# A softmax lookup convolution: three lookups of every slot between its logits and its numerators

## The chip, the cores and the metric

The kernel runs on one core of a Trainium2 chip. A core has five engines that run at the same time, each through its own list of instructions, and wait for one another through semaphores: TensorE (PE in the profile) multiplies matrices, VectorE (DVE), ScalarE (ACT) and GpSimd (POOL) work on elements, SyncE (SP) issues transfers. TensorE writes into PSUM, an accumulator memory of eight banks, from which VectorE or ScalarE must read the results before a bank can be written again.

The metric is the device time of one execution in microseconds (us), as the median of several.

## The reference, cut to what matters

The input has 16 images of 256 channels of 28 x 28 pixels. Each image is normalized by groups of 8 channels and goes through two "lookup convolutions". In such a convolution every channel has 16 centroids of 9 values. The 3 x 3 neighbourhood of a pixel in this channel is compared with the 16 centroids; a softmax over the negative squared distances gives 16 weights; the weighted mean of the centroids takes the place of the neighbourhood and is multiplied by the convolution's weights.

```python
def amm_conv3x3(x, centroids, w_sub):
    p = ...  # 9 neighbours of every pixel and channel: [B, N, C, 9]
    d = sum(p * p) - 2 * einsum('bncs,cks->bnck', p, centroids) + sum(centroids ** 2)
    attn = softmax(-d, axis=-1)                         # over the 16 centroids
    lut = einsum('cks,cso->cko', centroids, w_sub)
    return einsum('bnck,cko->bno', attn, lut)

out = amm_conv3x3(group_norm(x), centroids1, wsub1)
out = relu(batch_norm1(out))
out = amm_conv3x3(out, centroids2, wsub2)
out = batch_norm2(out)
out = squeeze_and_excite(out)
return x + relu(out + group_norm(x))
```

The kernel doesn't build `lut`. It computes the 16 exponentials of a channel, from them nine numerators (exponentials times centroids) and their sum, divides, and multiplies the nine quotients by `w_sub`. All is in fp32.

## The kernel before

The 256 channels are split into eight tiles of 32 channels (index m), and the 784 pixels into two parts of 384 and 400. One tile and one part are the work of one *slot*: there are 16 images x 2 convolutions x 2 parts x 8 tiles = 512 slots. In a slot TensorE makes three kinds of product:

- logits: 16 small products of 32 x 32 tiles, from patches `pt` and codes `wd` into two pairs of PSUM banks
- numerators: 16 small products, from the exponentials `e` and `cw` into two further pairs
- lookups: products of full width, from `q` (the quotients) and `ws` into the accumulators `acc0` and `acc1`; 36 for eight slots, so four or five a slot

Each product is two matmul records in the profile. PSUM's eight banks are two accumulators and a ring of three pairs:

```python
ring = [p_ring.tile([P, 2, 512], F32, name=f"pair{i}") for i in range(3)]
turn = [0]

def pair():
    turn[0] += 1
    return ring[turn[0] % 3]

def logits(u, rows):
    l, n = u["l"], u["px"][1]
    ps = [pair(), pair()]
    for t in range(4):
        for i in range(4):
            c = 32 * ctile(i, t)
            nc.tensor.matmul(                                       # L563
                ps[t // 2][c : c + 32, t % 2, :n],
                lhsT=wd[l][32 * i : 32 * i + rows, 4 * u["m"] + t, :],
                rhs=u["pt"][32 * i : 32 * i + rows, t, :n],
                start=True, stop=True,
            )
    return ps
```

What follows the logits of a slot, in the order of the data: two exponentials on ScalarE, one a pair; the numerators; two transposes and a reciprocal on VectorE; the division on GpSimd, for k and for the ninth row `tail`; a transpose back on VectorE; and, three slots later, the lookups.

```python
def b_exp(u):
    ...
    for ps in u.pop("lg"):
        e = epool.tile([P, 2, 400], F32, tag="e", name="e")
        nc.scalar.activation(e[:, :, :n], ps[:, :, :n], AF.Exp, scale=2.0)      # L621
        u["e"].append(e)

def b_num(u):
    ...
    u["nm"] = [pair(), pair()]
    for t in range(4):
        for i in range(4):
            c = 32 * ctile(i, t)
            nc.tensor.matmul(                                       # L631
                u["nm"][t // 2][32 * i : 32 * i + 32, t % 2, :n],
                lhsT=cw[l][c : c + 32, 4 * u["m"] + t, :],
                rhs=es[t // 2][c : c + 32, t % 2, :n],
                start=True, stop=True,
            )

def b_turn(u):
    ...
    for v, ps in enumerate(u.pop("nm")):
        nc.vector.transpose(nt[...], ps[...])                       # L643
    nc.vector.reciprocal(rc[:, : 8 * nb], u["nt"][:, :, SUM])       # L649
    ...

def c_scale(u):   # GpSimd: k = nt * rc (L659), tail (L665), extremes of sums (L671)
def c_turn(u):    # VectorE: q = transpose of k (L677), every fourth slot qt of tail (L684)
def c_look(u, o, h):
    ...
    nc.tensor.matmul(                                               # L695
        accs[key][:, :n], lhsT=ws[l][...], rhs=u["q"][h][:, :n], start=first, stop=last,
    )
    if last:
        evacuate(u, o, accs.pop(key))    # ScalarE: L707, L717
```

A plan puts every job into a slot and, in the slot, at a position; jobs are then issued in this order:

```python
LC = 3
LOOKS = [(m, o, h) for m in range(NQ) for o in range(2) for h in range(3 if m % 4 == 3 else 2)]
LOGITS, LOAD, MOVE, EXP, LOOK_A, NUM, TURN, SMALL, LOOK_B, MAX, LOOK_C, TURN_BACK, REST = range(13)
...
slots = [n0 + (LC + q) * self.step for q in range(NQ)]
more = [2 if (s, MAX) in self.jobs else 0 for s in slots]
k, room = 0, len(LOOKS) - sum(more)
for q, s in enumerate(slots):
    n = (q + 1) * room // NQ - q * room // NQ + more[q]
    for i, (m, o, h) in enumerate(LOOKS[k : k + n]):
        self.at(s, LOOK_A if i < n // 2 + n % 2 - more[q] // 2
                   else LOOK_B if i < n - more[q] else LOOK_C, c_look, of[m], o, h)
    k += n
```

So TensorE's order in a slot is logits, lookups A, numerators, small products (of the statistics and the gate), lookups B. In the second convolution the tiles 0 and 4 need the maximum of their logits ahead of time. For them logits are made six slots earlier at position MAX, and VectorE transposes them (z) and takes the maximum; such a slot gets two lookups more, at C, behind those early logits.

The number of lookups of a slot and how they lie before the change, over the whole run:

| lookups of the slot | A + B + C before | slots |
|---|---|---|
| 4 | 2 + 2 | 350 |
| 5 | 3 + 2 | 98 |
| 6 (early logits) | 2 + 2 + 2 | 34 |
| 7 (early logits) | 3 + 2 + 2 | 30 |

Of the kernel before, what the change touches and what calls it, by code (L numbers as in the profile page):

```python
# [69 lines left out]
def kernel(  # L70
# [655 lines left out]
    LOGITS, LOAD, MOVE, EXP, LOOK_A, NUM, TURN, SMALL, LOOK_B, MAX, LOOK_C, TURN_BACK, REST = range(13)  # L726

    class Plan:
# [13 lines left out]
        def emit(self):  # L742

            free = [-99] * len(pts)
            for slot, last, u in sorted(self.loads, key=lambda v: v[:2]):
                tile = free.index(min(free))
                assert free[tile] <= slot
                free[tile] = last
                self.at(slot, LOAD, patches, u, tile)
            for n0, of in self.tiles:  # L750
# [4 lines that stand above are left out]
                for q, s in enumerate(slots):  # L755
                    n = (q + 1) * room // NQ - q * room // NQ + more[q]
                    for i, (m, o, h) in enumerate(LOOKS[k : k + n]):
                        self.at(s, LOOK_A if i < n // 2 + n % 2 - more[q] // 2 else LOOK_B if i < n - more[q] else LOOK_C, c_look, of[m], o, h)
                    k += n
            for key in sorted(self.jobs):  # L760
                for f, a in self.jobs[key]:
                    f(*a)
# [234 lines left out]
```

## Time and profile before

| | before |
|---|---|
| median time of 3 runs | 2973.09 us (2972.99 to 2977.15) |
| span of the profiled run | 2969.2 us |
| mean granted TensorE clock | 0.989 |
| TensorE busy (matmul records) | 2871.6 us, 97% |
| VectorE busy | 2252.7 us, 76% |
| GpSimd busy | 1768.5 us, 60% |
| ScalarE busy | 1092.7 us, 37% |

A line of the groups gives the source line, the engine, the operation, what is written from what, the shapes, the number of instructions, then the busy time in us and the mean of one in ns, and last the engine's idle time ahead of them and what ended most of it. A line of the timeline gives the start in us, the time from the first start to the last end, the engine, the line and the operation, and how many instructions in a row it stands for; a wait ahead of it stands in brackets with what ended it. In the view of waits a line names who waited, for whom, the total in us, the times and the longest. Matmul records overlap, as TensorE is pipelined, and a record that stands inside a block of others is counted as busy time of the block.

### The profile page before, as it was taken

What the parts mean: (1) busy time and instruction counts of PE and PEld (TensorE: products, weight loads), DVE (VectorE), ACT (ScalarE), POOL (GpSimd) and SP (SyncE); (2) the same over time, 40 slices, a digit from 0 to 9 for tenths busy, and PEclk for the clock granted to TensorE, in tenths of its full rate; (3) what the DMA queues carried; (4) which work ended last, traced back from release to release, by engine and by line L of the source; (5) the groups of instructions that cost most, each with busy time, mean ns of one, the idle gap of its engine ahead of it and who ended that gap; (6) DMA issues with size and microseconds to landing.
All of it is one profiled execution on the core that took longest, in us unless ns stands there. A gap on an engine that the chain in (4) does not pass through costs nothing.

```text
span 2969.2 us, 94838 instructions
## 1 busy us (share of the span) xinstructions
PE 2871.6 (97%) x39834; PEld 1145.4 (39%) x39834; DVE 2252.7 (76%) x2760; ACT 1092.7 (37%) x1605; POOL 1768.5 (60%) x2583
## 2 busy tenths in 40 slices
PE   4999999999999999999999999999999999999995
PEld 2433333333333333333333333333333333334332
DVE  3476777787877878787787877878788787878884
ACT  1332343433434343343433434343343434333332
POOL 3474575666656566665656656566665656656553
PEclk8999999999999999999999999999999999999998
DMA  6877777767767676776767667676776767674641
GB/s 185 227 174 170 203 219 195 212 154 213 186 169 197 151 208 174 197 185 154 211 156 207 180 180 188 154 214 156 214 185 163 200 155 206 177 189 106 163 114 56
DMA packets 296773, 530.30 MB, mean 179 GB/s; under 512 B 94240, under 2 KB 251664, under 8 KB 296336
## 3 DMA queue, kind: packets, MB, share of 16 engines
q0 software_dynamic: 51648, 269.78, 34.9%
q1 hardware_dynamic: 242512, 251.70, 32.7%
q8 instruction: 316, 5.18, 0.7%
q10 hardware_dynamic: 2176, 2.65, 0.3%
q14 instruction: 121, 0.99, 0.1%
HBM read 269.96 MB, written 254.05 MB: 176 GB/s over the span
## 4 chain that ended last, share of the span: by engine, by line
PE 79%; DMA 7%; DVE 6%; POOL 4%; issue 2%; ACT 2%; SPq 0%; ACTq 0%; DVEq 0%; POOLq 0%
PE acc L695 47%; PE pair L631 16%; PE pair L563 14%; DMA xt<-in_x 4%; DVE nt L643 2%; POOL k L659 2%; DVE rc L649 1%; DVE gn_st L417 1%; POOL total L671 1%; DMA pt<-pat 1%; ACT e L621 1%; DMA ws<-dws 1%; PE pair L309 0%; PE pair L324 0%; DVE q L677 0%
## 5 line engine op out<-in xcount | busy, mean ns | idle before, releaser
L695 PE MATMUL acc<-q,ws 128*128 128x384 f32 (+1 forms) x4096 | 1641.0, 519 | 9.7 <-ACT y L717 9.7
L659 POOL TENSOR_TENSOR k<-nt,rc 128x832 f32<-128x832 f32 (+1 forms) x512 | 802.3, 1567 | 1132.9 <-DVE rc L649 1120.5
L643 DVE STREAM_TRANSPOSE nt<-pair 128x832 f32<-128x832 f32 (+1 forms) x1024 | 976.3, 992 | 603.5 <-PE pair L631 506.4
L621 ACT ACTIVATE e<-pair 128x800 f32<-128x800 f32 (+1 forms) x1024 | 787.8, 821 | 1358.8 <-PE pair L563 1357.3
L695 PEld LDWEIGHTS acc<-q,ws 128*128 128x128 f32 x4096 | 696.9, 189 | 907.7 <-issue 577.2
L631 PE MATMUL pair<-e,cw 32*32 32x384 f32 (+1 forms) x16384 | 580.3, 502 | 11.9 <-ACT e L621 10.6
L563 PE MATMUL pair<-pt,wd 19*32 19x384 f32 (+2 forms) x18432 | 561.0, 500 | 5.9 <-DMA pt<-pat 3.3
L677 DVE STREAM_TRANSPOSE q<-k 128x832 f32<-128x832 f32 (+1 forms) x512 | 489.1, 955 | 0.8 <-POOL k L659 0.8
L649 DVE RECIPROCAL rc<-nt 128x104 f32<-128x104 f32 (+1 forms) x512 | 398.5, 778 | 17.6
L631 PEld LDWEIGHTS pair<-e,cw 32*32 32x32 f32 x16384 | 167.5, 103 | 349.2 <-ACT e L621 321.4
L563 PEld LDWEIGHTS pair<-pt,wd 19*32 19x32 f32 (+1 forms) x18432 | 138.4, 103 | 340.1 <-issue 265.5
L665 POOL TENSOR_TENSOR tail<-nt,rc 128x104 f32<-128x104 f32 (+1 forms) x512 | 242.4, 473 | 0.0
L695 PE MATMUL acc<-qt,ws 128*128 128x400 f32 (+1 forms) x512 | 218.6, 509 | 0.0
L671 POOL TENSOR_TENSOR total<-total,nt 128x96 f32<-128x96 f32 (+1 forms) x448 | 198.7, 443 | 0.0
L468 POOL DMA_DIRECT2D pat<-side x280 | 186.6, 667 | 1.1 <-DMA pat<-im 0.7
L671 POOL TENSOR_TENSOR total<-total,rc 128x96 f32<-128x96 f32 (+1 forms) x448 | 175.5, 392 | 0.0
L695 PEld LDWEIGHTS acc<-qt,ws 128*128 128x128 f32 x512 | 90.8, 189 | 100.1 <-issue 50.6
L587 DVE TENSOR_REDUCE mx<-z 128x48 f32<-128x768 f32 (+1 forms) x128 | 120.8, 943 | 0.0
L582 DVE STREAM_TRANSPOSE z<-pair 128x768 f32<-128x768 f32 (+1 forms) x128 | 119.2, 969 | 0.0
L468 POOL DMA_DIRECT2D pat<-im x140 | 94.0, 672 | 3.5 <-ACT im L447 3.5
L707 ACT ACTIVATE im<-acc,bnsh,bnsc 128x384 f32<-128x384 f32 (+1 forms) x64 | 43.4, 678 | 139.4 <-PE acc L695 133.4
L717 ACT ACTIVATE y<-acc,bnsh,bnsc 128x384 f32<-128x384 f32 (+1 forms) x64 | 43.4, 679 | 91.7 <-PE acc L695 76.8
(106 smaller groups left out, 753.5 us busy)
## 6 DMA issues: line engine op xcount, KB each, us to landing
pat<-side POOLq DMA_DIRECT2D x232, 588.0 KB, 6.1
pt<-pat SPq DMA_DIRECT2D x1024, 112.5 KB
pt<-pat SPq DMA_DIRECT2D x1024, 108.0 KB
pat<-im POOLq DMA_DIRECT2D x116, 588.0 KB, 5.3
xt<-in_x POOLq DMA_DIRECT2D x32, 784.0 KB, 8.8
out_dram<-y POOLq DMA_DIRECT2D x16, 784.0 KB, 4.0
pat<-side POOLq DMA_DIRECT2D x24, 300.0 KB, 6.1
pat<-side POOLq DMA_DIRECT2D x24, 288.0 KB, 6.0
```

Of the source, the lines that this page charges most:

```text
L468: nc.gpsimd.dma_start(view(pat, (ROWS * p0 + 9 * k + 3 * dx) * HW + px, [[ROWS * HW, m], [HW, 3], [1, n]]), bass.AP(v.tensor, v.offset, [l ...
L563: nc.tensor.matmul(ps[t // 2][c : c + 32, t % 2, :n], lhsT=wd[l][32 * i : 32 * i + rows, 4 * u["m"] + t, :], rhs=u["pt"][32 * i : 32 * i + ...
L587: nc.vector.tensor_reduce(u["mx"][:, 2 * v : 2 * v + 2].rearrange("p t (j b) -> p t b j", j=2)[:, :, :nb], u["z"].pop(0)[:, : 64 * nb].rea ...
L621: nc.scalar.activation(e[:, :, :n], ps[:, :, :n], AF.Exp, scale=2.0)
L631: nc.tensor.matmul(u["nm"][t // 2][32 * i : 32 * i + 32, t % 2, :n], lhsT=cw[l][c : c + 32, 4 * u["m"] + t, :], rhs=es[t // 2][c : c + 32, ...
L643: nc.vector.transpose(nt[:, :nb, 2 * v : 2 * v + 2].rearrange("p b t r -> p t b r"), ps[:, :, : 32 * nb].rearrange("p t (b r) -> p t b r", ...
L649: nc.vector.reciprocal(rc[:, : 8 * nb], u["nt"][:, :, SUM])
L659: nc.gpsimd.tensor_tensor(q[:, :nb].rearrange("p b (a s) -> p (b a) s", s=8), nt[:, :, :8], rc.unsqueeze(2).to_broadcast([P, 8 * nb, 8]), ...
L665: nc.gpsimd.tensor_tensor(tails[key][:, :nb, 8 * (m % 4) : 8 * (m % 4) + 8], nt[:, :, 8].rearrange("p (b a) -> p b a", a=8), rc.rearrange( ...
L671: nc.gpsimd.tensor_add(t[:, : 8 * nb], t[:, : 8 * nb], v)
L677: nc.vector.transpose(q[:, :, : 32 * nb].rearrange("p h (b r) -> p h b r", r=32), u.pop("k")[:, :nb].rearrange("p b (h r) -> p h b r", h=2),)
L695: nc.tensor.matmul(accs[key][:, :n], lhsT=ws[l][:, 2 * m + h if h < 2 else 2 * NQ + m // 4, o * P : (o + 1) * P], rhs=u["q"][h][:, :n], st ...
```

## The change

The change sets how many lookups lie between the logits and the numerators. Before, the lookups of a slot, without those behind early logits, were halved, and an odd one went ahead of the numerators. Now three always go ahead of the numerators, and the others follow, whatever their number. This is meant to give the exponentials, which ScalarE makes from the logits, the time of three lookups before the numerators ask for them, in every slot.

```diff
                     for i, (m, o, h) in enumerate(LOOKS[k : k + n]):
-                        self.at(s, LOOK_A if i < n // 2 + n % 2 - more[q] // 2 else LOOK_B if i < n - more[q] else LOOK_C, c_look, of[m], o, h)
+
+                        self.at(s, LOOK_A if i < 3 else LOOK_B if i < n - more[q] else LOOK_C, c_look, of[m], o, h)
```

The lookups keep their order among themselves, and no instruction is added or taken away. The empty line in the diff moves the lines behind it by one.

## The prediction

> **What bounds the kernel now.** I read the busy table first, then the groups, the waits, and last the timeline, which tells more here than the others. From the page of the kernel before:
>
> ```profile
> PE 2871.6 (97%) x39834; PEld 1145.4 (39%) x39834; DVE 2252.7 (76%) x2760; ACT 1092.7 (37%) x1605; POOL 1768.5 (60%) x2583
> ...
> L631 PE MATMUL pair<-e,cw 32*32 32x384 f32 (+1 forms) x16384 | 580.3, 502 | 11.9 <-ACT e L621 10.6
> L563 PE MATMUL pair<-pt,wd 19*32 19x384 f32 (+2 forms) x18432 | 561.0, 500 | 5.9 <-DMA pt<-pat 3.3
> ```
>
> TensorE (PE) is 97% busy, so its stream sets the end. Of its 98 us without work (2969.2 - 2871.6) most lies in the first 60 us (40 us idle, by the table of windows) and the last 70 us (31 us idle). The view of waits says that TensorE hardly waits for the two engines this change is about:
>
> ```profile
> PE pair L631 <- ACT e L621: 10.6, 20, 6.4
> ...
> PE pair L563 <- DVE nt L643: 1.6, 5, 0.5
> ```
>
> But 580.3 us over 512 slots is 1.133 us for one block of numerators (L631, 32 matmul records), while a block of logits (L563), also 32 records, takes 561.0 / 576 = 0.974 us. So I looked at two neighbouring slots in the timeline. TensorE alone:
>
> ```profile
> 1013.82 1.56 PE L695 MATMUL acc<-q,ws 128*128 128x384 f32 x4
> 1015.31 1.14 PE L631 MATMUL pair<-e,cw 32*32 32x384 f32 x32
> 1016.38 1.56 PE L695 MATMUL acc<-q,ws 128*128 128x384 f32 x4
> 1017.87 0.93 PE L563 MATMUL pair<-pt,wd 19*32 19x384 f32 x32
> 1018.72 1.56 PE L695 MATMUL acc<-q,ws 128*128 128x384 f32 x4
> 1020.12 0.81 PE L695 MATMUL acc<-qt,ws 128*128 128x384 f32 x2
> 1020.86 0.93 PE L631 MATMUL pair<-e,cw 32*32 32x384 f32 x32
> ```
>
> A lookup is two records, so x4 is two lookups. Behind two lookups the numerators took 1.14 us, behind three 0.93 us. ScalarE in the first of these slots:
>
> ```profile
> 1014.01 1.51 ACT L621 ACTIVATE e<-pair 128x768 f32<-128x768 f32 x2 [3.39 <-PE pair L563]
> ```
>
> The second exponential ends at 1015.52, 0.21 us after the numerators began: their second half waits for it inside a block that counts as busy. In a block so stretched, the records of the second half start 53 ns after the exponential's end, and the block is longer by exactly the delay. I grouped all slots of the trace this way. Numerators behind two lookups: median 1.138 us, mean 1.152 (384 columns), and 1.168, mean 1.234 (400 columns). Behind three: median 0.928 and 0.954. This hidden wait is what the change removes.
>
> The timeline shows the opposite wait too, once, where VectorE came late:
>
> ```profile
> 1064.98 0.95 PE L631 MATMUL pair<-e,cw 32*32 32x400 f32 x32
> 1065.86 0.94 PE L695 MATMUL acc<-q,ws 128*128 128x400 f32 x2
> 1066.64 0.83 PE L695 MATMUL acc<-qt,ws 128*128 128x400 f32 x2
> 1067.40 0.90 PE L563 MATMUL pair<-pt,wd 19*32 19x400 f32 x16
> 1068.77 0.91 PE L563 MATMUL pair<-pt,wd 19*32 19x400 f32 x16 [0.47 <-DVE nt L643]
> ```
>
> VectorE at that time:
>
> ```profile
> 1067.71 1.93 DVE L643 STREAM_TRANSPOSE nt<-pair 128x832 f32<-128x832 f32 x2
> ```
>
> The logits split into x16 and x16: their second half goes into the pair of banks that holds the first half of the numerators just made, and may start only when the first of the two transposes has read it. There are three pairs, and a slot takes four (two for logits, two for numerators), so this holds in every slot. It is seldom felt, because two lookups stand in between.
>
> **What the Trainium skill says.** "Trainium Kernel Development and Optimization", Performance Expectations, warns that matmul busy time is a bad measure because matmuls are pipelined; the trace agrees, 1.14 against 0.93 us for the same 32 matmuls with no wait shown. "TensorE: Matmul & The Clock Gate", The mechanism, states that matmuls start and end in program order, without reordering; the trace agrees, as no L695 record passes the half-started logits at 1067.40. So a stall of the logits stalls the lookups behind them. "TensorEngine Tiling (Array Packing)", PSUM Bottleneck, says that tiling speeds up TensorE but not the evacuation of PSUM; here 0.93 us of packed numerators need two transposes of 0.90 to 0.97 us each.
>
> **The change part by part.** It adds and removes no instruction. By the plan's arithmetic, 350 slots of four lookups go from 2 + 2 around the numerators to 3 + 1. In 34 slots of six (those with early logits for the maxima), 2 + 2 + 2 become 3 + 1 + 2. The 98 slots of five (3 + 2) and 30 of seven (3 + 2 + 2) keep their order. So 384 slots change, 192 of each width.
>
> *What it removes.* A lookup takes 0.744 us at 384 columns (two of them from 1013.82 to 1015.31) and 0.77 at 400 (1.54 for two). Numerators begin that much later after their logits, and the second exponential, which ends 0.21 us after they begin now (median of both widths), will have ended over 0.5 us before. The whole stretch goes: 1.152 - 0.928 = 0.224 us at 384, 1.234 - 0.954 = 0.280 at 400. Gain: 192 x 0.224 + 192 x 0.280 = 97 us.
>
> *What it adds.* Time from the start S of a block of numerators. The first transpose of nt begins at S + 1.05 at 384 columns (medians of the slots; 1.08 at 400), once the first half is complete, and ends at S + 2.036 (2.130). This doesn't depend on how many lookups follow. TensorE, after an unstretched block, issues the next thing at S + 0.86 (1020.86 to 1021.71; 0.89 at 400). One lookup later, at S + 1.60 (1.655), come the logits, and their second half could issue 0.054 us behind the first. It must wait until the transpose's end plus 0.055 us (measured at 1068.77): S + 2.09 (2.185). Stall: 2.09 - 1.655 = 0.435 us, and 2.185 - 1.71 = 0.475 us. Before, two lookups and the stretch put the logits at S + 2.556 (2.638), medians, 0.5 us after the transpose.
> Loss: 192 x 0.435 + 192 x 0.475 = 175 us.
>
> *What it moves besides.* In the 34 slots with early logits, the ordinary logits after them take the pairs that hold nt's second half and z's first. VectorE does nt, nt, reciprocal and z in a row (from the end of the first: 0.95 + 0.78 + 0.96), so z's first is done near S + 4.75 to 4.9. TensorE now reaches those logits at about S + 4.4 to 4.6 (1.6 + 0.93 + 0.435 + two lookups of 1.5, less the overlap), so some 0.33 us more are lost: 34 x 0.33 = 11 us. In about 60 slots small matmuls (statistics, gates) stand between numerators and logits and cover perhaps 0.3 us of the new stall; three quarters of these slots change: -13 us. The lookups' own inputs are no issue: the third lookup is always of the tile three slots back, whose q was transposed more than a slot earlier.
>
> *Sum.* -97 + 175 + 11 - 13 = +76 us. With the mean of the transpose's end in place of its median (0.03 and 0.065 us later, for slots in which VectorE is busy with something else) it is 18 us more; a slower TensorE gives VectorE more slack, so I count a third: 2973 + 82 = **3055 us**.
>
> **Rivals.** (a) *The gain stands alone.* If VectorE's transposes ended in time, the kernel would gain 97 us: 2876. For it speaks that the wait for nt is only 1.6 us before and that VectorE is 24% idle. Against it: that idle time lies before the numerators are complete, and the transpose can start no sooner than S + 1.05. It alone takes 0.98 us, and one lookup of 0.74 us doesn't cover that. The event at 1068.77 shows this order is enforced.
> (b) *Gain and loss cancel.* If the stall were only about 0.25 us a slot, because the transpose begins sooner than the medians say, the time would stay near 2975. The medians, equal in both kinds of slot (1.053 and 1.080), speak against it.
> (c) *VectorE becomes the bound.* If its queue fell behind in the slots with maxima, gate and statistics, the stall would grow by up to 0.3 us in a quarter of the changed slots: 29 us more, about 3085. Against it: VectorE needs about 3.6 us of an ordinary slot of 5 us.
> (d) *The clock.* A TensorE that waits might be granted another clock. It was full between 560 and 2900 us, so nothing is to be gained, and the gaps are short.
>
> **Range and chances.** The two large terms, 97 and 175, come from medians of the same blocks, and the order of the waits is known; I trust their difference to about 25 us. Low end: half the expected surplus of stall, 3025. High end: rival (c), 3085. "Slower by over 2%" begins at 3032.6. Slower 0.82, within 2% 0.16, faster 0.02.
>
> **What would show it.** L631 should fall from 580 to about 485 us (1.133 to 0.95 us a slot). L563 should split into x16 and x16 or stretch to about 1.37 us in changed slots, its sum growing from 561 towards 650 to 730 us, with nt (L643) as the releaser. L695 should stay at 1641 us. VectorE's wait for L631 should grow. I'm wrong if the logits stay near 0.95 us behind one lookup, if nt starts well before S + 1.05, or if numerators behind three lookups still stretch.

## The result, and the profile after

| | before | after |
|---|---|---|
| median time | 2973.09 us | 3019.4 us (3019.26 to 3019.89) |
| ratio, 95% interval | | 1.0152 (1.0129 to 1.0175) |
| span of the profiled run | 2969.2 us | 3017.8 us |
| TensorE busy | 2871.6 us | 2908.9 us |
| numerators L631 | 580.3 us | 491.9 us |
| logits L563 | 561.0 us | 682.6 us |
| lookups L695 (q and qt together) | 1859.6 us | 1864.0 us |

The kernel became slower by 46 us, where 82 were predicted. The groups of the page after:

```profile
PE 2908.9 (96%) x39834; PEld 1150.9 (38%) x39834; DVE 2253.3 (75%) x2760; ACT 1098.2 (36%) x1605; POOL 1765.2 (58%) x2583
...
L563 PE MATMUL pair<-pt,wd 19*32 19x384 f32 (+2 forms) x18432 | 682.6, 501 | 9.9 <-DMA pt<-dm 5.2
L631 PE MATMUL pair<-e,cw 32*32 32x384 f32 (+1 forms) x16384 | 491.9, 502 | 6.5 <-ACT e L621 6.5
```

The numerators gave back 88 us and the logits took 122 us, in the same number of records with nearly the same mean. The waits of the matmuls (PE), on the other hand, hardly moved for either:

```profile
PE pair L434 <- POOL gn_dv L428: 15.6, 14, 1.1
...
PE pair L631 <- ACT e L621: 6.5, 3, 6.0
...
PE pair L563 <- DVE nt L643: 3.6, 6, 1.2
```

The first line grew most (4.2 us before): a small product of the statistics waits for GpSimd, 14 times. That is as much as TensorE's idle time grew in all (97.6 to 108.9 us), while other lines went up and down by up to 6 us. The weight loads of TensorE (PEld) do tell of the new wait. Who waited for VectorE's transposes, in the answers on line L643, before and after:

```profile
  PEld pair L563: 7.4, 11
```

```profile
  PEld pair L563: 86.9, 323
```

The weights of the logits had to wait for a transpose 323 times instead of 11; 334 changed slots have no small products between numerators and logits. How long the logits themselves are held, the timeline of TensorE shows. Two changed slots in a row:

```profile
1514.53 0.95 PE L631 MATMUL pair<-e,cw 32*32 32x400 f32 x32
1515.42 0.94 PE L695 MATMUL acc<-q,ws 128*128 128x400 f32 x2
1516.29 1.33 PE L563 MATMUL pair<-pt,wd 19*32 19x400 f32 x32
1517.55 2.28 PE L695 MATMUL acc<-q,ws 128*128 128x400 f32 x6
1519.76 0.95 PE L631 MATMUL pair<-e,cw 32*32 32x400 f32 x32
1520.65 0.94 PE L695 MATMUL acc<-q,ws 128*128 128x400 f32 x2
1521.52 1.38 PE L563 MATMUL pair<-pt,wd 19*32 19x400 f32 x32
```

VectorE in the first of them:

```profile
1515.61 1.98 DVE L643 STREAM_TRANSPOSE nt<-pair 128x832 f32<-128x832 f32 x2 [0.67 <-PE pair L631]
```

The logits take 1.33 and 1.38 us for what takes 0.95 us unstretched. Their first half starts at 1516.29, but the first of the two transposes ends only at 1516.66, and the second half starts 55 ns behind that. VectorE had been idle for 0.67 us, until the first numerators were there: it isn't late, the logits come too soon after the numerators.

Note where one lookup ends here: 1515.42 to 1516.29 is 0.87 us. The three ahead of the numerators take 1517.55 to 1519.76, 2.21 us, 0.74 us each. With 1.54 us for a block of two (median), each further lookup costs 0.67 us, and the first of a block 0.2 us more.

### The profile page after: what moved, and what is told of

It reads as the page before. It is cut to its first block, busy times and chain, and to the rows that moved or that the text cites. A ratio compares the mean times of both kernels' runs of the same rounds, so it can differ in the third digit from the quotient of the medians.

```text
span 3017.8 us, 94838 instructions
## 1 busy us (share of the span) xinstructions
PE 2908.9 (96%) x39834; PEld 1150.9 (38%) x39834; DVE 2253.3 (75%) x2760; ACT 1098.2 (36%) x1605; POOL 1765.2 (58%) x2583
## 4 chain that ended last, share of the span: by engine, by line
PE 87%; DMA 4%; POOL 3%; DVE 3%; issue 1%; ACT 0%; SPq 0%; ACTq 0%; DVEq 0%; POOLq 0%
PE acc L695 52%; PE pair L563 19%; PE pair L631 14%; DMA xt<-in_x 2%; POOL k L659 1%; DVE nt L643 1%; DMA pat<-im 1%; DMA pt<-dm 1%; DVE rc L649 1%; POOL total L671 1%; PE pair L324 1%; DMA dm<-mt 1%; PE pair L309 1%; POOL tail L665 0%; DVE gn_st L417 0%
## 5 line engine op out<-in xcount | busy, mean ns | idle before, releaser
L695 PE MATMUL acc<-q,ws 128*128 128x384 f32 (+1 forms) x4096 | 1649.0, 521 | 13.6 <-ACT y L717 9.3
L643 DVE STREAM_TRANSPOSE nt<-pair 128x832 f32<-128x832 f32 (+1 forms) x1024 | 977.4, 993 | 655.7 <-PE pair L631 493.0
L695 PEld LDWEIGHTS acc<-q,ws 128*128 128x128 f32 x4096 | 695.7, 190 | 926.6 <-issue 592.7
L563 PE MATMUL pair<-pt,wd 19*32 19x384 f32 (+2 forms) x18432 | 682.6, 501 | 9.9 <-DMA pt<-dm 5.2
L631 PE MATMUL pair<-e,cw 32*32 32x384 f32 (+1 forms) x16384 | 491.9, 502 | 6.5 <-ACT e L621 6.5
L563 PEld LDWEIGHTS pair<-pt,wd 19*32 19x32 f32 (+1 forms) x18432 | 186.2, 103 | 418.6 <-issue 251.8
L631 PEld LDWEIGHTS pair<-e,cw 32*32 32x32 f32 x16384 | 123.0, 103 | 298.1 <-issue 180.0
L695 PE MATMUL acc<-qt,ws 128*128 128x400 f32 (+1 forms) x512 | 215.0, 502 | 0.0
L695 PEld LDWEIGHTS acc<-qt,ws 128*128 128x128 f32 x512 | 93.6, 190 | 88.3 <-issue 28.9
```

Of the source, the lines that this page charges most:

```text
L563: nc.tensor.matmul(ps[t // 2][c : c + 32, t % 2, :n], lhsT=wd[l][32 * i : 32 * i + rows, 4 * u["m"] + t, :], rhs=u["pt"][32 * i : 32 * i + ...
L631: nc.tensor.matmul(u["nm"][t // 2][32 * i : 32 * i + 32, t % 2, :n], lhsT=cw[l][c : c + 32, 4 * u["m"] + t, :], rhs=es[t // 2][c : c + 32, ...
L643: nc.vector.transpose(nt[:, :nb, 2 * v : 2 * v + 2].rearrange("p b t r -> p t b r"), ps[:, :, : 32 * nb].rearrange("p t (b r) -> p t b r", ...
L695: nc.tensor.matmul(accs[key][:, :n], lhsT=ws[l][:, 2 * m + h if h < 2 else 2 * NQ + m // 4, o * P : (o + 1) * P], rhs=u["q"][h][:, :n], st ...
```

## The experiments

Theory A: the loss is the logits' second half, which waits until its pair of banks is read; so the time follows, one to one, the moment at which the pair comes free. Rival B: the new order costs by itself, by more expensive changes between small and wide products or by the lookups' inputs, whenever the pair comes free. The "pair free" column of the table below is the end of its last reader after the start of the numerators; "stretch" is the length of the logits beyond 0.928 (0.954) us. All are medians over the changed slots without early-logits blocks or small products between, for logits of 384 (400) columns. The edits are shown cut, with `...` for what is left out.

| order 3 + 1 | pair free | stretch of the logits | time |
|---|---|---|---|
| changed kernel | 2.035 (2.129) us | 0.340 (0.382) us | 3019.4 us |
| bank_copy_after | 2.149 (2.237) us | 0.451 (0.485) us | 3066.3 us |
| pair_copy_after | 1.780 (1.860) us | 0.083 (0.111) us | 2968.0 us |

### Two readers of the pair at once: bank_copy_after and bank_copy_before

```diff
-        for v, ps in enumerate(u.pop("nm")):
-            nc.vector.transpose(nt[... 2 * v : 2 * v + 2 ...], ps[...])
+        ps, ps1 = u.pop("nm")
+        cp = cpool.tile([P, 416], F32, tag="cp", name="cp")
+        nc.vector.transpose(nt[:, :nb, 0], ps[:, 0, ...])        # first bank
+        nc.scalar.copy(cp[:, : 32 * nb], ps[:, 1, : 32 * nb])    # second bank
+        nc.vector.transpose(nt[:, :nb, 2:4], ps1[...])
+        nc.vector.transpose(nt[:, :nb, 1], cp[...])
```

> The order of the changed kernel, but ScalarE copies the second bank of the first numerator pair to SBUF while VectorE transposes the first bank, so that the pair is free after some 0.5 us of reading instead of 1.0 us. Theory A (the whole loss is the logits' second half waiting for the first transpose behind one lookup): the logits shrink from 682.6 us back to about 560 us, the numerators stay at 492 us, and the time falls by about 110 us to 2905 us (2890 to 2925), below the kernel before. Rival B (the loss comes from the new order itself, such as more costly changes between wide and small products or the lookups' own inputs): the time stays above 2990 us.

Measured: 3066.3 us, ratio to before 1.0322 (1.0305 to 1.034). The expectation of theory A failed in its number, and the profile shows why: the copy didn't run beside the transpose. From the page of this kernel:

```profile
L646 ACT COPY cp<-pair 128x416 f32<-128x416 f32 (+1 forms) x512 | 252.3, 493 | 1147.8 <-DVE nt L645 1147.8
...
L564 PE MATMUL pair<-pt,wd 19*32 19x384 f32 (+2 forms) x18432 | 713.7, 501 | 30.7 <-ACT cp L646 15.0
L632 PE MATMUL pair<-e,cw 32*32 32x384 f32 (+1 forms) x16384 | 494.7, 501 | 8.3 <-ACT e L622 8.3
```

All of ScalarE's idle time ahead of the copy ended with VectorE's transpose of the other bank of the same pair: the program as built lets the second reader of the tile wait for the first. One after the other takes longer than one transpose, so the pair came free 0.11 us later than in the changed kernel, and the logits stretched by 0.11 and 0.10 us more. Over the 334 changed slots without small products that sums to 32 us in the trace, and the slots that the change left alone add 14 us; the time rose by 47 us. The edit turned out to be the opposite of what was meant, and its result speaks for A: the stretch followed the pair. By its number alone it fits rival B as well, which asked for more than 2990 us; the pair copy below decides.

> The same split reading of the first numerator pair, in the order of the kernel before. Theory A: two lookups already cover the transposes there, so nothing but the few late ones is gained: 2955 to 2975 us, the numerators still at about 580 us. If it gains as much as in the changed order (100 us or more), then the split reading helps for another reason and the pair of runs doesn't speak for theory A.

Measured: 2981.5 us, 1.0035 (1.0021 to 1.0049): the same later release of the pair costs 8 us behind two lookups and 47 us behind one. The logits (563.7 us) and the numerators (584.6 us) are nearly as in the kernel before. The expected 2955 to 2975 us was missed. As the edit delays the pair instead of hastening it, this tells the cost of a delay, and says nothing on whether a gain would have been absent.

### One reader, and an earlier release: pair_copy_after

```diff
-        for v, ps in enumerate(u.pop("nm")):
+        ps0, ps1 = u.pop("nm")
+        cp = cpool.tile([P, 2, 416], F32, tag="cp", name="cp")
+        nc.scalar.copy(cp[:, :, : 32 * nb], ps0[:, :, : 32 * nb])
+        for v, ps in ((1, ps1), (0, cp)):
             nc.vector.transpose(...)
```

> The order of the changed kernel, but ScalarE copies the whole first numerator pair to SBUF (one reader of that pair), and VectorE transposes the second pair first and the first from the copy. Theory A: the pair is free when the copy ends, some 0.82 us after its start, so at about 1.90 us after the numerators' start instead of 2.035 and 2.13 us; the wait of the logits' second half falls by about 0.15 and 0.21 us, 384 changed slots give 55 to 75 us, so 2945 to 2965 us, and a little more where ScalarE is busy with something else: 2945 to 2975 us. Rival B (ordering itself costs, not the time at which the pair comes free): 3010 us or more.

Measured: 2968.0 us, 0.9992 (0.9979 to 1.0006) of before, so 51 us less than the changed kernel in the same order. The pair comes free 0.255 and 0.269 us earlier, and the stretch shrinks by 0.257 and 0.271 us. The logits and the copy in the answer by groups:

```profile
L564 PE MATMUL pair<-pt,wd 19*32 19x384 f32 (+2 forms) x18432 | 605.9, 500 | 30.0 <-DMA pt<-dm 17.0 <-ACT cp L645 11.8 <-DMA pt<-pat 1.0
...
L645 ACT COPY cp<-pair 128x832 f32<-128x832 f32 (+1 forms) x512 | 422.8, 826 | 706.0 <-PE pair L632 705.8
```

The logits fell by 77 us against the changed kernel (682.6). The time fell by less, as TensorE's idle time grew from 108.9 to 129.8 us, above all in waits for statistics from VectorE (14.9 to 28.4 us) and for DMA (5.2 to 17.0 us). That the time lies in the expected range is partly luck: the pair came free earlier than the 1.90 us expected, and a smaller part of that reached the time. Rival B, which asked for 3010 us or more, is ruled out.

### No lookup at all between: four_then_none

```diff
-   LOOK_A if i < 3 else LOOK_B if i < n - more[q] else LOOK_C
+   LOOK_A if i < (4 if n - more[q] == 4 else 3) else LOOK_B if i < n - more[q] else LOOK_C
```

> Slots of four and six lookups: four ahead of the numerators and none between them and the next logits. Theory A with what the trace after shows, that a further lookup in a block costs 0.64 to 0.67 us and only the first of a block 0.87 us: the logits' second half begins when the first transpose ends, as with three, so every changed slot grows by one further lookup, 384 x 0.65 = 250 us, to about 3260 us. With the prediction's 0.744 to 0.77 us for every lookup: about 3305 us. Rival B: one change of product kind less a slot, so 3019 us or less.

Measured: 3247.1 us, 1.0926 (1.0904 to 1.0948); 228 us above the changed kernel. TensorE in one slot of it:

```profile
1508.11 0.95 PE L631 MATMUL pair<-e,cw 32*32 32x400 f32 x32
1508.81 1.15 PE L563 MATMUL pair<-pt,wd 19*32 19x400 f32 x16
1510.29 0.91 PE L563 MATMUL pair<-pt,wd 19*32 19x400 f32 x16 [0.34 <-DVE nt L643]
1511.13 2.85 PE L695 MATMUL acc<-q,ws 128*128 128x384 f32 x8
```

With more than a microsecond between the halves of the logits, the first half's records are over and the wait becomes visible, here 0.34 us of it. In the view of waits of this kernel it leads the list:

```profile
PE pair L563 <- DVE nt L643: 109.6, 333, 0.7
```

The second half of the logits still cannot start before the pair is free, so the fourth lookup ahead of the numerators is paid in full: 2.85 us of records instead of 2.20 (384 columns, medians). 228 us over 384 slots is 0.59 us, nearer to the 0.65 us of a further lookup than to the prediction's 0.744 to 0.77 us for any. Rival B asked for 3019 us or less and is ruled out here too. And the next kind of small product, without wide ones between, started 0.669 us (median, 384 columns) after the numerators' start instead of 0.857 us. So wide products behind a block of small ones start 0.19 us later than further small ones; what makes the difference isn't shown.

### The slots with early logits: max_slots_as_before

```diff
-   LOOK_A if i < 3 else ...
+   LOOK_A if i < (2 if n == 6 else 3) else ...
```

> The changed kernel, but the 34 slots of six lookups with early logits stay 2 + 2 + 2. The prediction counted 0.35 us of new wait, 0.33 us of waiting for z and 0.2 us of gain for each of them, so about 16 us: 3003 us by its reckoning. If these slots cost no more than the others (0.08 to 0.12 us each): 3015 to 3017 us.

Measured: 3004.1 us, 1.0106 (1.0087 to 1.0126), 15 us below the changed kernel: 0.45 us for each of the 34 slots, near the sum that the prediction counted, but not by its terms. The trace of the changed kernel shows in these slots 0.36 us of stretch on the early logits (12.2 us in all) and 0.2 us (median; 7.0 us in all) on the ordinary logits behind them, which wait for z. So the wait for z is smaller than counted, and the gain that was to be given up is not given up: in this run the numerators behind two lookups are not stretched in these slots (0.2 us in all, against 6.3 us in the kernel before). Their logits stand behind one lookup of the slot ahead and are stretched by 0.42 us (median), while the first exponential starts 1.05 us after the logits' start in this kernel and in the kernel before. So the second exponential ends 0.19 us before the numerators start, where it ended 0.19 us after it. The two waits are not independent: a stall of the logits is time for the exponentials too.

### A lookup cut in two: cut_lookup and cut_lookup_136

If two lookups are 0.21 us too few for the exponentials and one is 0.3 us too few for the transpose, then the right place lies within the third lookup. In slots of four of the kernel before, that lookup is cut by columns (in the first slot of a group, where `k` is 0, the second lookup):

```diff
+    CUT = 160
...
+                        if n == 4:
+                            cut = 1 if k == 0 else 2
+                            if i == cut:
+                                if k:
+                                    self.at(s, LOOK_A, c_look, of[m], o, h, 0, CUT)
+                                    self.at(s, LOOK_B, c_look, of[m], o, h, CUT, None)
...
-            accs[key][:, :n], lhsT=ws[l][...], rhs=u["q"][h][:, :n], start=first, stop=last,
+            accs[key][:, c0:c1], lhsT=ws[l][...], rhs=u["q"][h][:, c0:c1], start=first, stop=last,
```

> In the 350 slots of four lookups one lookup is cut by columns: 160 columns go ahead of the numerators and the other 224 or 240 follow, so 2.4 + 1.6 lookups; slots of six as before. Theory A: both waits vanish (the exponentials need 0.21 us more than two lookups give, the transpose leaves about 0.3 us to spare), numerators at about 490 us, logits at about 560 us; the cut costs two more matmul records and weight loads, 0.06 to 0.13 us a slot, so 2915 to 2945 us. Rival B (any move of work ahead of the numerators costs): at or above 2973 us.

Measured: 2937.1 us, 0.9881 (0.9865 to 0.9898) of before, so 1.2% faster than the kernel before, and faster than the changed one. TensorE in one slot and the next logits of it:

```profile
1517.82 0.93 PE L563 MATMUL pair<-pt,wd 19*32 19x384 f32 x32
1518.67 1.83 PE L698 MATMUL acc<-q,ws 128*128 128x384 f32 x6
1520.43 0.93 PE L631 MATMUL pair<-e,cw 32*32 32x384 f32 x32
1521.29 1.29 PE L698 MATMUL acc<-q,ws 128*128 128x224 f32 x4
1522.51 0.93 PE L563 MATMUL pair<-pt,wd 21*32 21x384 f32 x32
```

Numerators and logits both take 0.93 us: neither is stretched. From the page:

```profile
L563 PE MATMUL pair<-pt,wd 19*32 19x384 f32 (+2 forms) x18432 | 586.1, 500 | 14.9 <-DVE nt L643 9.2
L631 PE MATMUL pair<-e,cw 32*32 32x384 f32 (+1 forms) x16384 | 509.9, 503 | 8.3 <-ACT e L621 8.3
```

70 us come off the numerators and 25 us go onto the logits. Neither sum is as low as expected (490 and 560 us), because of slots where ScalarE or VectorE is late for other reasons: the numerators behind a third lookup or a piece of one have means of 0.974 and 1.020 us against medians of 0.928 and 0.954, and in 96 of the 101 logits blocks that are stretched by over 0.05 us the first transpose began late. The cut costs little: all lookups take 1867.4 us, 8 us more than before, for 350 more pieces.

> As the kernel with the cut lookup, but the cut lies at 136 columns instead of 160, and the 34 slots of six are cut too (2 and a part, the rest and 1, then 2). Theory A: 136 columns last 136 x 4 / 2.4 = 0.227 us by the pace of the lookups (384 columns in 0.64 us), still over the 0.21 us that the exponentials lack; the logits lose less time, as the rest is longer. 5 to 15 us better than with 160: 2922 to 2932 us. If the margin for the exponentials is too small, the numerators stretch again and it is 2937 us or more.

Measured: 2933.7 us, 0.9887 (0.9855 to 0.9919). The numerators take 512.5 us and the logits 585.0 us, as with 160 columns. The expected 2922 to 2932 us was just missed. The interval holds the former result, so this doesn't settle whether the other place of the cut or the six-lookup slots gave anything. For the latter the trace with 160 columns left little to gain: the numerators of those slots were stretched by 0.3 us in all.

## Why the prediction was wrong

The direction and both mechanisms were right, and the slowdown was there; its size was 46 us instead of 82 us, inside the 2% that was given 0.16, and below the range. Term by term (the profiled runs differ by 48.5 us):

| term | predicted | change in the traces |
|---|---|---|
| numerators no longer stretched | -97 us | -88 us |
| logits behind one lookup, and behind small products | +175 - 13 us | +118 us in all changed slots (7 us before, 125 after) |
| logits waiting for z | +11 us | +4 us (3 us before, 7 after) |
| late transposes | +6 us | in the lines above |
| lookups | none | +4 us |
| TensorE idle | not counted | +11 us |

**The step that failed** is in "What it adds": "One lookup later, at S + 1.60 (1.655), come the logits". They came at S + 1.700 (1.753), by the medians of the numerators of 384 (400) columns. The prediction took 0.744 and 0.77 us for a lookup, half of the time of a block of two. But a block of n lookups isn't n times a lookup. The trace after gives 0.87 us for a block of one, and the third of three adds 0.67 us at 400 columns. The prediction's own lines had shown it: its block of three, 1018.72 to 1020.86, took 2.14 us and its block of two 1.49 us, so the third cost 0.65 us and the first 0.84 us. Moving a lookup from one block to the other moves only a further lookup. The one that stays carries the block's fixed part, which covers 0.1 us more of the transpose than I thought. So the stretch was 0.340 (0.382) us instead of 0.435 (0.475). Over the 334 changed slots without small products between, that is 334 x 0.095 = 32 us of the 44 us by which this line of the table was too large; 7 us more are stretch that these slots had before the change as well. The smaller misses nearly cancel, by luck: z and the late transposes came out lower, by 7 and 6 us, the other three lines higher, by 9, 4 and 11 us.

**The gain** was over-sized by 9 us: I took it that the whole stretch of the numerators goes. In slots in which ScalarE has other work ahead of the exponentials, three lookups don't suffice either; the mean stays at 0.946 and 0.979 us, against medians of 0.928 and 0.954. In 30 of the 32 blocks that are still stretched by over 0.05 us, ScalarE came to the exponentials straight from another line.

**What held.** The transpose's times counted from the numerators' start (2.036 and 2.130 us before, 2.035 and 2.129 after) didn't move with the number of lookups. The stretch ran one to one with the release of the pair, shown by three kernels; the time followed it in part (51 us of the 88 us by which the stretch of the 334 slots shrank with the pair copy). In 48 changed slots small products covered most of the stall (mean 0.067 us left instead of 0.366), so 48 x 0.3 = 14 us, against 13 predicted. The slots with early logits cost in sum what was counted, by terms that weren't.

**Smaller faults.** The wait of VectorE for the numerators (L643 for L631), which was to grow, went from 506.4 to 493.0 us. A transpose takes 0.94 to 0.98 us at 384 columns and 1.00 to 1.05 us at 400, not 0.90 to 0.97 us; no term rests on that reading. And half of the surplus of 82 us would have put the low end of the range near 3014 us, not 3025.

**The rivals.** (a) was wrong about this order, but the cut lookup shows 70 of its 97 us on the numerators, once the transpose is mostly covered as well. (b) is the nearest of the rivals in time and wrong in kind: gain and loss don't cancel, and the transpose doesn't begin sooner. (c) didn't happen: VectorE idled before the transposes as ever, and its busy time is unchanged. (d) played no part: the mean clock is 0.987, against 0.989.

**The statistics.** The 11 us for which the small product L434 waits longer don't come from a slower GpSimd. In 13 of the 14 places it starts some 7.3 us after the numerators of the slot ahead, no later than in the kernel before (medians 7.27 after, 7.47 before). But the numerators of its own slot start 5.20 us after those, instead of 6.29: four lookups lie between the two blocks, where five did.

**What stays open.** It isn't shown whether two readers of one pair, freed from waiting for each other, would read it faster.

## What to carry to other kernels

Work ahead of a product covers the wait for the engine that feeds it, and work behind it covers the wait for the engine that frees its buffer; what is given to the first is taken from the second. Measure both margins from the same event, and if neither whole step fits, cut the step: here a piece of 160 of 384 columns took both waits out of most slots. And take what a moved instruction costs from the difference between blocks of n and n + 1, never from a block's mean, as the block's fixed part stays where it is.

## What the runs showed of the hardware

Behind a block of small products (32 x 32 tiles) a wide product started 0.857 us after the block's start, and a further block of small ones 0.669 us: 0.19 us for the change. The way back added about as much: from the start of one lookup of 384 columns to the next small products it took 0.843 us, where each further lookup of a block added 0.645 us (medians of the changed kernel). The prediction's S + 0.86 held the first of these costs; the second is the fixed part that it spread over the lookups.

The new wait of some 0.35 us a slot on TensorE left almost no trace in the waits of the matmuls (3.6 us shown of some 122 us), because the records of the first half cover it. It shows in the length of the block, and its releaser in the waits of the weight loads. For the wait of the numerators, the page of the kernel before had it:

```profile
L631 PEld LDWEIGHTS pair<-e,cw 32*32 32x32 f32 x16384 | 167.5, 103 | 349.2 <-ACT e L621 321.4
```

These 321.4 us name the engine, not the loss: the numerators were stretched by 98.5 us in all.
